# Two expert blocks moved behind the result's copy, with their rows summed on chip

## The chip, the core and the metric

The kernel runs on one core of a Trainium2 chip. A core has engines with an instruction queue each: PE (TensorE: matrix products, with PEld for its weight loads), DVE (VectorE), ACT (ScalarE), POOL (GpSimd) and SP (SyncE, which only starts transfers). Sixteen DMA engines move data between the chip's memory (DRAM) and the on-chip memory (SBUF). The engines run on their own and meet through semaphores. The metric is the device time of the whole program in microseconds (us), measured per execution; the median of the executions is what is compared.

## The reference

A layer of a graph network on 3125 nodes with 256 features. A graph part and a mixing part are added to `x`; then each node passes through two of eight expert networks, and their weighted results are added:

```python
x = x + gnn(xn, edges) + mix(xn)
xt = layernorm(x)
probs = softmax(xt @ Wr + br)                 # 8 experts
top_p, top_idx = top_k(probs, 2)
weights = top_p / top_p.sum(-1)
xe = norm(xt) * ln_g[e] + ln_b[e]             # for each expert e
h = gelu(xe @ W1[e] + b1[e])                  # 256 -> 1024
y = h @ W2[e] + b2[e]                         # 1024 -> 256
out = x + sum over the two chosen e of weights[e] * y[e]
```

Everything is in float32. What matters here is the last sum: a node's result is its row of `x` plus two expert rows, which come from two different experts, and so at two different times.

## The kernel before

Up to about 715 us the kernel computes the graph and mixing parts (lines 215 to 770). For 25 tiles of 126 nodes it then stores the sum so far into `acc_dram`, a DRAM tensor of 3125 + 128 rows (L773), finds the two experts of each node, and scatters the node's normalised row, with its eight expert weights and its number, into `xs_dram` (L872). There every expert has a region of its own, filled beforehand with blank rows whose number is 3125 (`blank`, L491 to 493), so that the results of unused slots go to the spare rows of `acc_dram`.

A plan (from L897) counts the rows that each expert holds, and lists blocks of 256 rows (`SB`): each of the eight experts has a first block with a fixed place, and what goes beyond is listed in `begin_i`, `who_i` (whole blocks) and `hbegin_i`, `hwho_i` (half blocks of 128). `used_i` holds how many of each the plan came to.

The expert stage is the function `block` (from L969), called 28 times in a row: first the eight fixed blocks, then sixteen listed ones, and after each four of these one half block. A call

- loads the two weight matrices of its expert, 1 MB each (L992, L993), and a bias (L995); the buffers of these are three deep (`ew`);
- loads its rows `xs` from `xs_dram` (L1006; three buffers). A listed block takes place and expert from registers, which SP reads from the plan (L985);
- transposes the rows on PE (L1010), scales them on DVE into `xe` (L1014; two buffers), multiplies by the first matrix with a GELU on ACT (L1020, L1022), and by the second (L1033), in halves of 128 rows;
- for each half adds the bias (L1036), multiplies by the row's weight (L1037), and adds the 128 rows into `acc_dram` with an indirect DMA that POOL issues (L1038). It adds in memory, and each of these waits until the one before has landed, since both may touch one row.

After the 28 calls come blocks that this input does not need, under three `If`s (L1049 to L1055) on `used` and `hused`, which every engine reads from `used_i` into a register (L1047, L1048). An engine that skips a body still has to raise the semaphores that the body would have raised. The last line copies `acc_dram` to `out` (L1056, 3.2 MB).

The kernel is written with a framework (Tile) that places the semaphores and chooses the order of each engine's queue from a plan of its own, in which an instruction goes out when its inputs and buffers are free; the order of the queues is therefore not that of the text. By hand an order can be asked for: `tc.issue_after(ins)` keeps what is written under it behind `ins` on the same engine, and `tc.add_manual_dep` makes one instruction wait for another. `declare_no_dep` drops waits between the members of a group.

Of the kernel before, what the change touches and what calls it, by code (L numbers as in the profile page):

```python
# [9 lines left out]
F32 = mybir.dt.float32  # L10
I32 = mybir.dt.int32
# [3 lines left out]
OP = mybir.AluOpType  # L15
AX = mybir.AxisListType

N = 3125
C = 256
# [10 lines left out]
NE = 8  # L30
HID = 1024
KF = HID // 128
# [10 lines left out]
SURE = 2 * N // SB  # L43
HSURE = NE // 2
# [19 lines left out]
def gps_layer(  # L64
# [9 lines left out]
    nc = tc.nc  # L74
# [11 lines left out]
    def ps_tr():  # L86
        return psum.tile([128, 512], F32, tag="tr", name="ps_tr", bufs=2)
# [17 lines left out]
    acc_dram = dram.tile([N + 128, C], F32, name="acc_dram")  # L105
# [385 lines left out]
    blank = mp.tile([128, ROW], F32, name="blank", bufs=1)  # L491
    nc.gpsimd.memset(blank, 0.0)
    nc.gpsimd.iota(blank[:, C + NE:].bitcast(I32), pattern=[[0, 1]], base=N, channel_multiplier=1)
    xs_b = xs_dram.rearrange("(n p) c -> p n c", p=128)
    nb = XROWS // 128
    FILL = 53
# [4 lines left out]
    nh = TB * HEADS  # L501
# [392 lines left out]
    with tc.tile_pool(name="plan", bufs=1) as lp:  # L894
# [63 lines left out]
        nc.vector.tensor_scalar(hgone, hwho[:, :, 0], float(NE - 1), None, op0=OP.min)  # L958
        hwho_i = keep.tile([128, NE], I32, name="hwho_i")
        nc.vector.tensor_copy(hwho_i, hgone)  # L960
        used_i = keep.tile([128, 2], I32, name="used_i")
        nc.vector.tensor_copy(used_i[:, 0:1], ends[:, 0, NE - 1:])
        nc.vector.tensor_copy(used_i[:, 1:2], hends[:, 0, NE - 1:])


    SP = (mybir.EngineType.SP,)
    NH = SB // 128
    with tc.tile_pool(name="ffn", bufs=2) as fp:
        def block(b, half=False):  # L969

            nh = 1 if half else NH
            ns = 128 * nh
            if b < NE and not half:
                begin, e = b * R, b
                xs_b, w1_b, w2_b = xs_dram[begin:begin + SB, :], W1[e], W2[e]
                b2_b = b2[e:e + 1, :]
                is_e = None
            else:
                if half:
                    of, is_e = (hbegin_i, hwho_i), is_hwho[:, b:b + 1, :]  # L980
                    j = b
# [12 lines left out]
            b2s = ew.tile([128, C], F32, name="b2s")  # L994
            nc.sync.dma_start(b2s, b2_b.to_broadcast([128, C]))  # L995
            if is_e is None:
                sm = small[:, :, b]
            else:
                all_ = fp.tile([128, KS, NE], F32, name="all_")
                nc.vector.tensor_tensor(all_, small,  # L1000
                                        is_e.to_broadcast([128, KS, NE]), OP.mult)
                sm = fp.tile([128, KS], F32, name="sm")
                nc.vector.tensor_reduce(sm, all_, AX.X, OP.add)
            lng, lnb, b1s = sm[:, :KC], sm[:, KC:2 * KC], sm[:, 2 * KC:]
            xs = fp.tile([128, NH, ROW], F32, name="xs", bufs=3)[:, :nh, :]
            nc.sync.dma_start(xs, xs_b.rearrange("(h p) c -> p h c", p=128))  # L1006
            pt = ps_tr()
            for k in range(KC):
                for h in range(nh):
                    nc.tensor.transpose(pt[:, k * ns + h * 128:k * ns + h * 128 + 128],  # L1010
                                        xs[:, h, 128 * k:128 * k + 128], ident)
            xe = fp.tile([128, KC, SB], F32, name="xe")[:, :, :ns]
            for k in range(KC):
                nc.vector.tensor_scalar(xe[:, k, :], pt[:, k * ns:(k + 1) * ns],  # L1014
                                        lng[:, k:k + 1], lnb[:, k:k + 1], op0=OP.mult, op1=OP.add)
            hf = fp.tile([128, KF, SB], F32, name="hf")[:, :, :ns]
            for m in range(KF):
                pm = ps_mm()[:, :ns]
                for k in range(KC):
                    nc.tensor.matmul(pm, w1[:, k, 128 * m:128 * m + 128], xe[:, k, :],  # L1020
                                     start=(k == 0), stop=(k == KC - 1))
                nc.scalar.activation(hf[:, m, :], pm, AF.Gelu, bias=b1s[:, m:m + 1])  # L1022
            for h in range(nh):
                if is_e is None:
                    gate = xs[:, h, C + e:C + e + 1]
                else:
                    gate = fp.tile([128, 1], F32, name="gate", bufs=4)
                    scr = fp.tile([128, NE], F32, name="scr", bufs=4)
                    nc.vector.scalar_tensor_tensor(scr, xs[:, h, C:C + NE], 1.0, is_e[:, 0, :],  # L1029
                                                   op0=OP.mult, op1=OP.mult, accum_out=gate)  # L1030
                po = ps_o()[:, :C]
                for m in range(KF):
                    nc.tensor.matmul(po, hf[:, m, 128 * h:128 * h + 128], w2[:, m, :],  # L1033
                                     start=(m == 0), stop=(m == KF - 1))
                y = fp.tile([128, C], F32, name="y", bufs=4)
                nc.vector.tensor_tensor(y, po, b2s, OP.add)  # L1036
                nc.vector.tensor_scalar(y, y, gate, None, op0=OP.mult)  # L1037
                nc.gpsimd.indirect_dma_start(  # L1038
                    out=acc_dram[:, :],
                    out_offset=bass.IndirectOffsetOnAxis(ap=xs[:, h, C + NE:].bitcast(I32), axis=0),  # L1040
                    in_=y, in_offset=None, compute_op=OP.add)

        for b in range(SURE):
            block(b)
            if b >= NE and (b - NE) % HSURE == HSURE - 1:
                block((b - NE) // HSURE, half=True)
        used = nc.values_load(used_i[0:1, 0:1], min_val=0, max_val=ND)  # L1047
        hused = nc.values_load(used_i[0:1, 1:2], min_val=0, max_val=NE)  # L1048
        for b0, b1 in ((SURE, SURE + 2), (SURE + 2, NBLK)):  # L1049
            with tc.If(used > b0 - NE):  # L1050
                for b in range(b0, b1):
                    block(b)
        with tc.If(hused > HSURE):
            for b in range(HSURE, NE):
                block(b, half=True)  # L1055
    nc.sync.dma_start(out, acc_dram[:N, :])  # L1056


# [57 lines left out]
```

## Time and profile before

| | |
|---|---|
| median of 3 runs | 1149.16 us (1146.96 to 1151.12) |
| the profiled execution, its time | 1149.45 us |
| its span (first to last instruction) | 1147.7 us |
| granted PE clock, mean of the span | 0.968 |
| PE busy | 1057.1 us (92%) |
| DVE, ACT, POOL busy | 553.6, 427.5, 169.7 us |
| a whole block on PE: L1020, L1033 | 7.07 us each |
| a half block on PE: L1020, L1033 | 3.73, 3.62 us |
| adding DMA (L1038): POOL's time, start to landing | 1.54 us; 3.7 / 4.2 / 7.7 us (shortest, median, longest) |
| scatter into `xs_dram` (L872): the same | 0.98 us; 2.6 / 2.8 / 10.0 us |
| gather into `near` (L283): the same | 0.97 us; 3.1 / 4.2 / 5.3 us |
| last adding DMA starts | 1126.5 us |
| copy to `out` is issued | 1133.7 us |

How to read it: the page shows busy times of the engines, not who waits for whom. A busy time counts towards the span only where nothing else runs beside it. Of the stage of interest the useful views are the timeline of one engine, whose brackets give the idle time before an instruction and what ended it; the waits of an engine's queue; and, for one line of the program, the list of its queue events (branches, semaphore steps, drains), which are not counted as busy. The 40-slice rows of the page show the end of the program at a glance:

```profile
PE   5799999999999999999999998299999999899992
...
DMA  7884965963007521213121111157666676666734
```

In these rows a slice is 28.7 us. PE is at nine tenths or more through the expert stage, and in the last slice, where the copy runs, at two.

### The profile page before, as it was taken

To read this page: it belongs to the slowest core of one execution; us is meant where nothing else is said; L and a number is where in the kernel's file an instruction comes from. 1 tells how busy PE (TensorE), PEld (TensorE's weight loads), DVE (VectorE), ACT (ScalarE), POOL (GpSimd) and SP (SyncE) were. 2 spreads that over 40 slices of the span, in tenths; PEclk is the share of its full clock that TensorE was granted. 3 is DMA by queue.
4 is the path that set the end of the run, shared out by engine and by line. 5 is a ranking of instruction groups with operands and counts; after the bars stand their busy time and mean duration, and the time that the engine had idled before them with its cause. 6 is when DMAs were issued, how large, how long until landed. Compare 5 with 4: busy or idle time off the path is not lost. (4 is left out here: it accounts for less than half of the span.)

```text
span 1147.7 us, 15551 instructions
## 1 busy us (share of the span) xinstructions
PE 1057.1 (92%) x5613; PEld 807.3 (70%) x5613; DVE 553.6 (48%) x1767; ACT 427.5 (37%) x936; POOL 169.7 (15%) x153
## 2 busy tenths in 40 slices
PE   5799999999999999999999998299999999899992
PEld 2357988988996454545454557288888888788881
DVE  5757788788761184848383937411112222222210
ACT  3454755755732233334333336122222232222220
POOL 2220000000001002020202021212212222122221
PEclk9889999999999999999999999599999999999996
DMA  7884965963007521213121111157666676666734
GB/s 230 293 278 131 252 168 130 253 170 96 1 1 239 176 91 38 91 38 91 38 91 37 36 38 46 52 147 201 188 193 189 187 235 184 201 188 193 227 65 126
DMA packets 121148, 161.43 MB, mean 141 GB/s; under 512 B 9570, under 2 KB 109320, under 8 KB 120870
## 3 DMA queue, kind: packets, MB, share of 16 engines
q1 hardware_dynamic: 108156, 144.40, 41.0%
q0 software_dynamic: 12064, 15.08, 7.1%
q8 instruction: 49, 0.80, 0.3%
q10 hardware_dynamic: 840, 0.83, 0.2%
q14 instruction: 39, 0.32, 0.1%
HBM read 101.37 MB, written 62.10 MB: 142 GB/s over the span
## 5 line engine op out<-in xcount | busy, mean ns | idle before, releaser
L747 PE MATMUL ps_mm<-hT,wih 128*128 128x504 f32 (+1 forms) x672 | 257.8, 543 | 1.6 <-ACT act L749 1.6
L747 PEld LDWEIGHTS ps_mm<-hT,wih 128*128 128x128 f32 x672 | 120.3, 190 | 133.8 <-issue 127.9
L1020 PE MATMUL ps_mm<-xe,w 128*128 128x256 f32 (+1 forms) x896 | 189.4, 369 | 3.3 <-DVE xe L1014 3.3
L1033 PE MATMUL ps_o<-w,hf 128*128 128x256 f32 x832 | 184.2, 379 | 0.0
L1020 PEld LDWEIGHTS ps_mm<-xe,w 128*128 128x128 f32 x896 | 161.6, 192 | 27.0 <-DVE xe L1014 6.6
L630 PE MATMUL ps_o<-A,hi 126*128 126x252 f32 (+1 forms) x650 | 176.3, 305 | 0.8 <-ACT A L392 0.7
L1033 PEld LDWEIGHTS ps_o<-w,hf 128*128 128x128 f32 x832 | 157.8, 190 | 21.3
L630 PE MATMUL ps_o<-A,lo 126*128 126x252 f32 (+1 forms) x650 | 161.2, 281 | 0.0
L1022 ACT ACTIVATE hf<-ps_mm,sm 128x256 f32<-128x256 f32 (+1 forms) x160 | 71.7, 453 | 199.2 <-PE ps_mm L1020 197.5
L392 ACT CAST A<-ps_mm 126x450 fp32r<-126x450 f32 x175 | 93.8, 538 | 99.8 <-PE ps_mm L390 98.2
L1038 POOL DMA_INDIRECT acc_dram<-y,xs x52 | 80.4, 1546 | 318.8 <-DVE scr L1029 131.6
L630 PEld LDWEIGHTS ps_o<-A,hi 126*128 126x128 f32 x650 | 124.9, 192 | 2.8 <-ACT aggT L638 1.7
L384 DVE TENSOR_TENSOR hr<-two,rowT 128x756 bf16<-128x756 bf16 x175 | 95.9, 548 | 62.9 <-PE ps_mm L390 62.4
L630 PEld LDWEIGHTS ps_o<-A,lo 126*128 126x128 f32 x650 | 125.2, 193 | 0.0
L390 PE MATMUL ps_mm<-hk,hr 128*126 128x150 bf16 x1050 | 102.2, 233 | 12.7 <-DVE hk L384 12.4
L384 DVE TENSOR_TENSOR hk<-two,keyT 128x900 bf16<-128x900 bf16 x175 | 108.8, 622 | 0.0
L390 PEld LDWEIGHTS <-hr 128*126 128x126 bf16 x1050 | 91.2, 137 | 18.7 <-DVE hk L384 16.5
L1036 DVE TENSOR_TENSOR y<-ps_o,b2s 128x256 f32<-128x256 f32 x52 | 22.1, 425 | 163.9 <-PE ps_o L1033 163.9
L749 ACT ACTIVATE act<-ps_mm,bg 128x504 f32<-128x504 f32 (+1 forms) x84 | 52.6, 634 | 107.3 <-PE ps_mm L747 107.2
L795 DVE SCALAR_TENSOR_TENSOR scr<-xl,wrows 126x256 f32<-126x256 f32 x160 | 75.5, 472 | 3.3
L872 POOL DMA_INDIRECT xs_dram<-rows,at_i x50 | 52.6, 1052 | 127.9 <-DVE at_i L869 110.9
L1022 ACT ACTIVATE hf<-ps_mm,small 128x256 f32<-128x256 f32 x64 | 29.8, 474 | 76.4 <-PE ps_mm L1020 76.4
(250 smaller groups left out, 920.1 us busy)
## 6 DMA issues: line engine op xcount, KB each, us to landing
w<-in_W_dram SPq DMA_DIRECT2D x56, 1024.0 KB
xs_dram<-blank SPq DMA_DIRECT2D x3, 7022.5 KB
xs_dram<-blank SPq DMA_DIRECT2D x1, 6757.5 KB
xs<-xs_dram SPq DMA_DIRECT2D x24, 265.0 KB
root_dram<-hr SPq DMA_DIRECT2D x24, 252.0 KB
root<-root_dram SPq DMA_DIRECT2D x6, 1008.0 KB
b2s<-in_b_dram SPq DMA_DIRECT2D x28, 128.0 KB
xn_dram<-xn SPq DMA_DIRECT2D x5, 630.0 KB
```

Source lines behind the costliest of these rows:

```text
L384: row = nc.vector.tensor_tensor(to[:, :m], two[:, :, :w, :].to_broadcast([128, m, w, GH]), of[:, g:g + m, None, :].to_broadcast([128, m, w ...
L390: mm = nc.tensor.matmul(pa[:P, i * DT:(i + 1) * DT], hr[:, i, :, h], hk[:, i, :, h], start=(h == 0), stop=(h == GH - 1))
L392: copy = nc.scalar.copy(A[:, :, c0:c0 + m * D], pa[:P, :m * DT].rearrange("p (d t) -> p t d", t=T))
L630: last = nc.tensor.matmul(pg[k][:, :n], of[:, t, 128 * k:128 * k + 128], A[:, t, :n], start=(t == 0 and of is hi), stop=(t == T - 1 and of ...
L747: mm = nc.tensor.matmul(pm[:, :n], wih[:, k, i, 128 * m:128 * m + 128], hT[:, k, :n], start=(k == 0), stop=(k == KH - 1))
L749: nc.scalar.activation(act[:, i, :n], pm[:, :n], AF.Tanh if gate == 2 else AF.Sigmoid, bias=bg[:, gate, m:m + 1])
L795: nc.vector.scalar_tensor_tensor(scr, xl[:, i, :], 1.0, wrows[:, e, :], op0=OP.mult, op1=OP.mult, accum_out=lg[:, i, e:e + 1])
L872: put = nc.gpsimd.indirect_dma_start(out=xs_dram[:, :], out_offset=bass.IndirectOffsetOnAxis(ap=at_i[:w, i:i + 1], axis=0), in_=rows[:w, i ...
L1020: nc.tensor.matmul(pm, w1[:, k, 128 * m:128 * m + 128], xe[:, k, :], start=(k == 0), stop=(k == KC - 1))
L1022: nc.scalar.activation(hf[:, m, :], pm, AF.Gelu, bias=b1s[:, m:m + 1])
L1033: nc.tensor.matmul(po, hf[:, m, 128 * h:128 * h + 128], w2[:, m, :], start=(m == 0), stop=(m == KF - 1))
L1038: nc.gpsimd.indirect_dma_start(out=acc_dram[:, :], out_offset=bass.IndirectOffsetOnAxis(ap=xs[:, h, C + NE:].bitcast(I32), axis=0), in_=y, ...
```

## The change

- The loop of 28 calls leaves out the blocks of experts 6 and 7; they are called after it, with `last=True`.
- The first of the two, in its own body, copies `acc_dram` to `out`: the copy now stands ahead of their results. It waits for all the adding DMAs before it.
- A `last` block gathers, for its 256 rows, what has been summed so far into `old`: expert 6 from `acc_dram`, expert 7 from `out`, after expert 6's rows have landed there. The gather from `out` leaves out rows whose number is beyond 3124, hence the `memset`.
- In place of the multiplication and the adding DMA, one DVE operation forms `y * gate + old`, and an indirect DMA without addition stores the rows in `out`. Each waits for the copy; among each other they don't wait. Expert 7's gathers wait for expert 6's stores.
- The plan also counts `more`: whether there are whole blocks beyond the sixteen or halves beyond the four. If so, the results of experts 6 and 7 are also added to `acc_dram` in the old way, the further blocks run as before, and `acc_dram` is copied to `out` once more at the end. These are two new `If`s, one ahead of the three and one behind.
- The registers are read behind the last matmul, the last row operation and the last stores of their engines.
- The spare rows of `acc_dram` are set to zero once, in the mixing stage.

```diff
@@ in the mixing stage
     nc.gpsimd.iota(blank[:, C + NE:].bitcast(I32), pattern=[[0, 1]], base=N, channel_multiplier=1)
+    nc.sync.dma_start(acc_dram[N:, :], blank[:, :C])
@@ in the plan
-        used_i = keep.tile([128, 2], I32, name="used_i")
-        nc.vector.tensor_copy(used_i[:, 0:1], ends[:, 0, NE - 1:])
-        nc.vector.tensor_copy(used_i[:, 1:2], hends[:, 0, NE - 1:])
+        used_f = lp.tile([128, 3], F32, name="used_f")
+        nc.vector.tensor_copy(used_f[:, 0:1], ends[:, 0, NE - 1:])
+        nc.vector.tensor_copy(used_f[:, 1:2], hends[:, 0, NE - 1:])
+        spill = lp.tile([128, 2], F32, name="spill")
+        for i, sure in enumerate((SURE - NE, HSURE)):
+            nc.vector.tensor_scalar(spill[:, i:i + 1], used_f[:, i:i + 1], -float(sure), 0.0,
+                                    op0=OP.add, op1=OP.max)
+        nc.vector.tensor_tensor(used_f[:, 2:], spill[:, 0:1], spill[:, 1:2], OP.add)
+        used_i = keep.tile([128, 3], I32, name="used_i")
+        nc.vector.tensor_copy(used_i, used_f)
@@ in block(b, half=False, last=False), after the load of xs
+            if last:
+                if not done:
+                    done.append(nc.sync.dma_start(out, acc_dram[:N, :]))
+                old = fp.tile([128, NH, C], F32, name="old", bufs=2)
+                sums, most = (acc_dram, None) if len(done) == 1 else (out, N - 1)
+                if most:
+                    nc.vector.memset(old, 0.0)
+                for h in range(nh):
+                    get = nc.gpsimd.indirect_dma_start(
+                        out=old[:, h, :], out_offset=None, in_=sums[:, :],
+                        in_offset=bass.IndirectOffsetOnAxis(
+                            ap=xs[:, h, C + NE:].bitcast(I32), axis=0),
+                        bounds_check=most, oob_is_err=False)
+                    for put in done[1:]:
+                        after(get, put)
@@ in block, after y = po + b2s
+                ys.append(y)
+                if not last:
+                    nc.vector.tensor_scalar(y, y, gate, None, op0=OP.mult)
+                    add(y, h, xs)
+                    continue
+                new = fp.tile([128, C], F32, name="new", bufs=2)
+                row = nc.vector.scalar_tensor_tensor(new, y, gate, old[:, h, :], op0=OP.mult, op1=OP.add)
+                put = nc.gpsimd.indirect_dma_start(
+                    out=out[:, :],
+                    out_offset=bass.IndirectOffsetOnAxis(ap=xs[:, h, C + NE:].bitcast(I32), axis=0),
+                    in_=new, in_offset=None, bounds_check=N - 1, oob_is_err=False)
+                tc.declare_no_dep(put.ins, group="lasts", reason="rows of their own")
+                tc.add_to_no_dep_group("lasts", put.ins)
+                after(put, done[0])
+                puts.append(put)
+            done.extend(puts)
+            return xs, ys, (*puts, row, mm) if last else ()
@@ the calls
-        for b in range(SURE):
+        done = []
+        for b in (*range(NE - 2), *range(NE, SURE)):
             block(b)
             if b >= NE and (b - NE) % HSURE == HSURE - 1:
                 block((b - NE) // HSURE, half=True)
-        used = nc.values_load(used_i[0:1, 0:1], min_val=0, max_val=ND)
-        hused = nc.values_load(used_i[0:1, 1:2], min_val=0, max_val=NE)
+        lasts = [block(b, last=True) for b in (NE - 2, NE - 1)]
+        with ExitStack() as queued:
+            for ins in lasts[-1][2]:
+                queued.enter_context(tc.issue_after(ins.ins))
+            used, hused, more = [nc.values_load(used_i[0:1, i:i + 1], min_val=0, max_val=ND)
+                                 for i in range(3)]
+        with tc.If(more > 0):
+            for e, (xs, ys, _) in zip((NE - 2, NE - 1), lasts):
+                for h in range(NH):
+                    nc.vector.tensor_scalar(ys[h], ys[h], xs[:, h, C + e:C + e + 1], None,
+                                            op0=OP.mult)
+                    add(ys[h], h, xs)
...
-    nc.sync.dma_start(out, acc_dram[:N, :])
+        with tc.If(more > 0):
+            again = nc.sync.dma_start(out, acc_dram[:N, :])
+            for put in done:
+                after(again, put)
```

`add(y, h, of)` is the adding DMA of before (L1038) as a function; `after(ins, of)` makes `ins` wait for `of` with `tc.add_manual_dep`.

More of the change, by code (lines that the diff above doesn't have):

```diff
@@ L968, in gps_layer, with add, block @@
     with tc.tile_pool(name="ffn", bufs=2) as fp:
-        def block(b, half=False):
+        def add(y, h, of):
+            nc.gpsimd.indirect_dma_start(
+                out=acc_dram[:, :],
+                out_offset=bass.IndirectOffsetOnAxis(ap=of[:, h, C + NE:].bitcast(I32), axis=0),
+                in_=y, in_offset=None, compute_op=OP.add)
+        def block(b, half=False, last=False):
             nh = 1 if half else NH
@@ L1006, in block @@
             nc.sync.dma_start(xs, xs_b.rearrange("(h p) c -> p h c", p=128))
+            if last:
[13 more added lines that the diff above has]
+                        after(get, put)
+            ys, puts = [], []
             pt = ps_tr()
@@ L1032, in block, with after @@
                 for m in range(KF):
-                    nc.tensor.matmul(po, hf[:, m, 128 * h:128 * h + 128], w2[:, m, :],
-                                     start=(m == 0), stop=(m == KF - 1))
+                    mm = nc.tensor.matmul(po, hf[:, m, 128 * h:128 * h + 128], w2[:, m, :],
+                                          start=(m == 0), stop=(m == KF - 1))
                 y = fp.tile([128, C], F32, name="y", bufs=4)
                 nc.vector.tensor_tensor(y, po, b2s, OP.add)
-                nc.vector.tensor_scalar(y, y, gate, None, op0=OP.mult)
-                nc.gpsimd.indirect_dma_start(
-                    out=acc_dram[:, :],
-                    out_offset=bass.IndirectOffsetOnAxis(ap=xs[:, h, C + NE:].bitcast(I32), axis=0),
-                    in_=y, in_offset=None, compute_op=OP.add)
-        for b in range(SURE):
+                ys.append(y)
[7 more added lines that the diff above has]
+                    out=out[:, :],
+                    out_offset=bass.IndirectOffsetOnAxis(ap=xs[:, h, C + NE:].bitcast(I32), axis=0),
+                    in_=new, in_offset=None, bounds_check=N - 1, oob_is_err=False)
[5 more added lines that the diff above has]
+            return xs, ys, (*puts, row, mm) if last else ()
+        def after(ins, of):
+            tc.add_manual_dep(ins.ins, of.ins.name, mybir.DependencyInfo(
+                mybir.DependencyClass.Sync, mybir.DependencyReason.DATA), reason="rows of one another")
+        done = []
+        for b in (*range(NE - 2), *range(NE, SURE)):
             block(b)
```

## The prediction

> **What bounds the kernel now.** I read the page's group table first, then the TensorE (PE) timeline of the expert stage, then the tail after the last matmul; the change touches only the last two. From 740 us to 1125.4 PE runs the 28 calls of `block` almost without a break:
>
> ```profile
> L1020 PE MATMUL ps_mm<-xe,w 128*128 128x256 f32 (+1 forms) x896 | 189.4, 369 | 3.3 <-DVE xe L1014 3.3
> L1033 PE MATMUL ps_o<-w,hf 128*128 128x256 f32 x832 | 184.2, 379 | 0.0
> ```
>
> The last figures are PE's idle time before those lines: 3.3 and 0.0 us. So a term counts only if it opens a gap on PE or lies behind its last matmul. The PE timeline has one real gap. Columns are start, length, what, and in brackets the idle time and its releaser:
>
> ```profile
> 981.95 3.73 PE L1020 MATMUL ps_mm<-xe,w 128*128 128x128 f32 x32
> 985.52 3.62 PE L1033 MATMUL ps_o<-w,hf 128*128 128x256 f32 x16
> 988.98 0.60 PE L1010 MATMUL ps_tr<-ident,xs 128*128 128x128 f32 x4
> 992.72 0.67 PE L1010 MATMUL ps_tr<-ident,xs 128*128 128x128 f32 x4 [3.15 <-DMA xs<-xs_dram]
> 993.75 8.59 PE L1020 MATMUL ps_mm<-xe,w 128*128 128x256 f32 x32 [0.35 <-DVE xe L1014]
> ...
> 1067.17 7.07 PE L1033 MATMUL ps_o<-w,hf 128*128 128x256 f32 x32
> 1074.08 1.04 PE L1010 MATMUL ps_tr<-ident,xs 128*128 128x128 f32 x8
> 1075.32 7.17 PE L1020 MATMUL ps_mm<-xe,w 128*128 128x256 f32 x32 [0.20 <-DVE xe L1014]
> ```
>
> Transposes run in pairs of calls: eight (or six, with a half) stand ahead of the first call's L1020. At 992.72 the pair's second `xs` was not there. `xs` has three buffers, so it is loaded only after the scatter of three calls earlier has landed: that scatter started at 984.34, 2.2 us after its block's last matmul, and landed at 989.87; the load was issued at 989.96 and arrived at 992.7. Normally two further whole blocks cover this; here one of the two was a half block, 7 us instead of 14.
>
> The tail is this: the SyncE waits (line, what it waited for, total, times, longest), then events of the tail by line (durations, first and last start):
>
> ```profile
> SPq L1056 <- DMA acc_dram<-y,xs: 31.1, 1, 31.1
> SPq L1112 <- DMA out_dram<-acc_dram: 11.7, 1, 11.7
> ```
>
> ```profile
> L1050 PEldq COMPARE_BRANCH  x2: 2287/3610/4933, 1123.8 to 1126.3; - x2
> ...
> L1050 POOLq INC_SWDGE_SEM  x2: 915/916/917, 1127.7 to 1131.1; - x2
> ```
>
> ```profile
> L1053 PEldq COMPARE_BRANCH  x1: 2642/2642/2642, 1131.9 to 1131.9; - x1
> ```
>
> ```profile
> L1112 POOLq DRAIN  x3: 46/107/3139, 1133.7 to 1147.4; - x3
> ...
> L1112 PEldq DRAIN  x2: 8/8/8, 1140.7 to 1147.2; - x2
> ```
>
> Last matmul 1125.4; last scatter 1126.5, landed 1131.1 (POOL's own wait on it ends there). The copy starts only at 1133.7: POOL (GpSimd) walks three skipped `If`s, each with a 0.92 us semaphore step, and the copy waits for the last one. It ends at 1146.5, 12.7 us later, and 1.2 us of closing steps end the span. From last matmul to end: 22.3 us.
>
> **The change, part by part.**
>
> *The copy moved forward.* It is issued after the 26th call's scatter. Number the calls 0 to 27: halves were 12, 17, 22, 27 and become 10, 15, 20, 25; blocks 6 and 7 become 26 and 27. Call T0 the end of call 25. Its scatter starts at T0+1.1 and lands 4.6 later (tail rows), so the copy runs from T0+5.8 to T0+18.5, beside some 33 us of PE work. Gain: the 12.7 us leave the tail, and so does the wait before them. If uncovered, they come back whole.
> It is queued on SyncE, where it could hold up block 7's loads. This queue does not follow the program's text: the weights of the first blocks were issued at 360 to 377 us, before inputs that stand earlier in the code, and the read of `used` at 726.3, before the first `xs` at 736.9. What is ready goes first. Block 7's weights are free to load when call 24 releases its buffers and its `xs` when that call's scatter lands, 13 and 6 us ahead of the copy; so I put the copy behind them, at no cost.
>
> *A new gap.* Call 24 is a block, 25 a half, (26, 27) a pair: the same pattern as (16, 17), (18, 19) now. The old gap recurs at (16, 17), whose predecessor 15 is a half. Today the fourth half ends the chain and nothing follows it; now a pair does. Price from the rows: from the half's end to L1020 4.61 us (989.14 to 993.75) against 1.08 (1074.24 to 1075.32), +3.53; and that L1020 took 8.59 against 7.17, +1.42: together **+4.95**. [...] Bounds: 0, if the queue puts block 7's transposes later; 7, if the landing takes the 7.7 us that is the longest of these scatters.
>
> *Gathers, sums and plain stores* in blocks 6 and 7. Four gathers, no row with 1 KB rows from this place: nearest are `near` (0.97 us of POOL, 4.2 to landing) and the plain store `xs_dram` (0.99, 2.8). Four plain stores replace four adding scatters (1.54, 4.2). I take 1.0 and 2.8, ends 1.0/2.8 and 1.5/4.2. Block 6's gathers go at T0+5.8; even slowed to 8 us by the copy they precede the first new sum at T0+16.8. Its stores wait for the copy (T0+18.5) and for its last row (T0+21.3, with the gap); landed at T0+24 to 25.5; block 7's gathers wait behind them on POOL and land at T0+28 to 31.4. They are needed at T0+34.4. Three us spare, cost 0. Without the gap the need is at T0+30.4, and up to 1 us shows. The `new` operation is 0.47 us (a 126x256 SCALAR_TENSOR_TENSOR row, L795) instead of 0.35: +0.12 in the tail. The `old` memset and the missing gate multiply are off the path.
>
> *Plan and blank store.* About four DVE operations of 0.15 us more, ending near 730.6 instead of 730.0, and a third register load of some 0.7 us on SyncE; the first `xs` waits for scatters until 736.5 anyway. Without that cover, 1.3 us. The 128 KB store to `acc_dram` goes out some 300 us before anyone adds there: 0.
>
> *The tail.* Two more skipped `If`s, and the third register load on each engine. From the last matmul, in us:
> POOL: rows, sum and issue of the last store 1.0; eight waits of 0.085, 1.7; three loads of 0.38, 2.9; four skips of 1.6 (1127.35 to 1128.94 is one), 9.3; 0 to 0.6 more if the last store lands after the second skip asks for it; the fifth, which has no GpSimd work, 0.3: about 9.9; DRAIN 3.1: **13.0**.
> PE: now its third branch ends 9.2 after the last matmul. One load more and two near branches make 9.9. Its DRAIN came 6.1 us later, behind a 16 KB instruction packet that started only at 1138.2, amid the copy; such a packet otherwise costs 2.3 to 2.6 us (the 2.29 and 2.64 rows), so 12.4.
> Then 0.85 of closing: **13.8 instead of 22.3**, gain 8.5. [...] Ends of the tail: 10.5 if POOL's DRAIN shrinks and PE has its last packet early; 15.5 if both new `If`s cost PE 0.8 each.
>
> **Sum.** +4.95 − 8.5 = −3.6 us (3.55). Span 1147.7 → 1144.1. The profiled execution took 1149.45, 1.75 around its span; so 1145.9, and the runs' median lies 0.29 below that execution: **1145.6 us**, 0.31% under the median of 1149.16. The gain of the copy is half eaten by the pattern it creates.
>
> **Rivals.**
> *No new gap.* If the transposes of 27 stand behind L1020 of 26, or its `xs` comes early, only the tail counts: −8.5, 1140.7. For it: blocks 6 and 7 need no register-read addresses. Against it: the half/pair pattern is the same, and `xs` still waits for a scatter.
> *The chain copy, store, gather, store becomes late.* For it: four dependent transfers, and adding scatters took up to 7.7 us, `xs_dram` stores up to 10. If block 6's last store takes 7.7 and block 7's gather 10, its rows come at T0+40.5 rather than 34.4: +6.1, 1151.7; at half that excess, 1148.7. It decides once the gathers land after T0+34.4.
> *The copy stands ahead of block 7's loads on SyncE*: the slower side. SyncE then sits in its wait until T0+5.8; weights and `xs` (2.4 MB) queue behind the copy to T0+18.5 and at some 0.35 MB/us land near T0+25.5. Since the pair's transposes wait for that `xs`, block 6 itself starts at T0+26.5 rather than T0+4.6: +22, 1167. It decides as soon as block 7's `xs` arrives later than T0+3.6; each us after that is a us. Against it: the order by readiness shown above.
>
> **From these to the numbers.** Forecast 0.50, own range 1142.5 to 1148.5; no gap 0.22 (1138.5 to 1142.5); late chain 0.16 (1148.5 to 1154); queue order 0.08; others, slower, 0.04. The bound of 0.3% is 3.4 us, about what a measurement of this kernel can tell from no change, so faster means under 1145.7: half of the first case and the second, 0.47. Within: the other half and half of the third, 0.33. Slower: 0.20. Range 1139 to 1152: all of the first, most of the second, half of the third.
>
> **What would show it.** Copy issued about 30 us before the last matmul and ended before block 7's first L1020 is half done; SyncE's loads of block 7 before it; a PE wait of 3 us for `xs` ahead of block 6, and L1020 of 8.6 after it; DVE never waiting for `old` in block 7; the end 13 to 14 us after the last matmul, with POOL's DRAIN and PE's nearly together. It is wrong if DVE or POOL waits on gathers at the end, if PE's branches take other times, or if the pairing changes.

## The result, and the profile after

| | before | after |
|---|---|---|
| median of the runs | 1149.16 us (5 runs, 1146.96 to 1151.12) | 1142.23 us (5 runs, 1138.13 to 1143.33) |
| profiled execution, its span | 1149.45, 1147.7 us | 1143.33, 1141.5 us |
| granted PE clock, mean | 0.968 | 0.972 |
| last matmul ends | 1125.39 us | 1128.30 us |
| from there to the end | 22.3 us | 13.2 us |

By the medians that is 6.9 us less, where 3.6 was forecast (1145.6 us); the ratio of the runs is 0.9931, with an interval of 0.9909 to 0.9954, which is 5.3 to 10.5 us. The profiled execution is the slowest of the five of after, so the traces account for 6.2 us and not 6.9.

The PE row of the page, 40 slices of 28.5 us:

```profile
PE   5799999999999999999999998199999998999995
```

The last digit was 2 and is 5. The one 8 among the last 9s is the old gap: it stood a slice later in the row of before, where the expert stage was at 9 but for this slice and the last. The new gap is too short to lower its digit. The PE timeline of the changed kernel shows it: first the place where the old gap now is, then the end of the stage. Columns are start, length, what, idle time and its releaser.

```profile
955.56 3.62 PE L1067 MATMUL ps_o<-w,hf 128*128 128x256 f32 x16
959.01 0.60 PE L1044 MATMUL ps_tr<-ident,xs 128*128 128x128 f32 x4
962.94 1.12 PE L1044 MATMUL ps_tr<-ident,xs 128*128 128x128 f32 x4 [3.33 <-DMA xs<-xs_dram]
963.96 9.76 PE L1054 MATMUL ps_mm<-xe,w 128*128 128x256 f32 x32
```

```profile
1093.16 3.62 PE L1067 MATMUL ps_o<-w,hf 128*128 128x256 f32 x16
1096.62 0.60 PE L1044 MATMUL ps_tr<-ident,xs 128*128 128x128 f32 x4
1100.01 0.66 PE L1044 MATMUL ps_tr<-ident,xs 128*128 128x128 f32 x4 [2.80 <-DMA xs<-xs_dram]
1100.50 7.07 PE L1054 MATMUL ps_mm<-xe,w 128*128 128x256 f32 x32
...
1121.23 7.07 PE L1067 MATMUL ps_o<-w,hf 128*128 128x256 f32 x32
```

L1044, L1054 and L1067 are the L1010, L1020 and L1033 of before. A second wait for `xs` has appeared, ahead of the pair of blocks 6 and 7, and nothing else interrupts PE until it is done: no wait for a weight, a gather or the copy.

SyncE's queue shows why the copy (L1027) disturbs nothing. Block 7's two weights (L1008, L1009), bias (L1011) and rows (L1022) are all issued ahead of it:

```profile
1082.88 0.37 SPq L1008 DMA_DIRECT2D w<-in_W_dram  x1
1089.78 0.37 SPq L1009 DMA_DIRECT2D w<-in_W_dram  x1
1090.24 0.54 SPq L1011 DMA_DIRECT2D b2s<-in_b_dram  x1
1097.39 0.37 SPq L1022 DMA_DIRECT2D xs<-xs_dram  x1
1102.18 0.60 SPq L1027 DMA_DIRECT2D out_dram<-acc_dram  x1
```

POOL's timeline of the same stretch holds the chain of gathers (L1033) and plain stores (L1079):

```profile
1102.43 1.04 POOL L1033 DMA_INDIRECT old<-acc_dram,xs  x1 [2.54 <-DMA acc_dram<-y,xs]
1103.77 0.98 POOL L1033 DMA_INDIRECT old<-acc_dram,xs  x1 [0.31 <-issue]
1115.50 1.02 POOL L1079 DMA_INDIRECT out_dram<-new,xs  x1 [10.75 <-DVE y L1070]
1116.82 1.00 POOL L1079 DMA_INDIRECT out_dram<-new,xs  x1 [0.30 <-issue]
1120.44 1.04 POOL L1033 DMA_INDIRECT old<-out_dram,xs  x1 [2.62 <-issue]
1121.79 1.03 POOL L1033 DMA_INDIRECT old<-out_dram,xs  x1 [0.30 <-issue]
1126.26 1.00 POOL L1079 DMA_INDIRECT out_dram<-new,xs  x1 [3.44 <-DVE new L1078]
1129.56 1.00 POOL L1079 DMA_INDIRECT out_dram<-new,xs  x1 [2.29 <-DMA out_dram<-new,xs]
```

The last store starts 1.26 us after the last matmul's end: the two DVE operations behind that matmul end at 1129.28, 0.28 us before the store. The bracket names another releaser, the landing of the store before (1129.45), which came at nearly the same time; in e9 below the distance is the same 1.27 us, and there the bracket names `new`. DVE's waits agree that no gather was late: it waited for `old` once, 3.1 us in block 6 by this view, which cost PE nothing, and never in block 7.

```profile
DVE new L1078 <- DMA old<-acc_dram,xs: 3.1, 1, 3.1
```

The tail, in the queue events of the skipped `If`s and of the end, by line (durations shortest, median, longest; first and last start):

```profile
L1107 POOLq INC_SWDGE_SEM  x1: 1022/1022/1022, 1131.0 to 1131.0; - x1
```

```profile
L1114 PEldq COMPARE_BRANCH  x2: 430/1904/3378, 1126.2 to 1128.5; - x2
...
L1114 POOLq INC_SWDGE_SEM  x2: 983/994/1006, 1132.8 to 1134.3; - x2
```

```profile
L1117 PEldq COMPARE_BRANCH  x1: 4068/4068/4068, 1132.5 to 1132.5; - x1
...
L1117 POOLq INC_SWDGE_SEM  x1: 1001/1001/1001, 1136.0 to 1136.0; - x1
```

```profile
L1179 POOLq DRAIN  x3: 51/107/3466, 1137.2 to 1141.3; - x3
...
L1179 PEldq DRAIN  x2: 8/8/8, 1137.1 to 1141.0; - x2
```

POOL pays four semaphore steps of about 1.0 us, one for each skipped body that has GpSimd work, then, from 1137.2, the DRAIN of 3.47 us. PE is through its five branches at 1137.1, 3.5 us before POOL's DRAIN ends: POOL sets the end.

The account of the two profiled executions, span 1147.7 to 1141.5, from the timelines:

| | forecast | measured |
|---|---|---|
| stage begins (738.25, was 739.96), its first 12 matmuls (4.80 us, was 4.00) | 0 | −0.9 |
| the old gap at its new place (wait 3.33, L1054 9.76; were 3.15 and 8.59) | 0 | +1.3 |
| the new gap: 1096.78 to 1100.50 is 3.72, less the normal 1.08, and L1054 0.1 shorter than normal | +4.95 | +2.5 |
| the tail | −8.5 | −9.1 |
| sum | −3.6 | −6.2 |

### The profile page after: what moved, and what is told of

Its sections match the earlier page's. It is cut to its first block, busy times and chain, and to the rows that moved or that the text cites. A ratio compares the mean times of both kernels' runs of the same rounds, so it can differ in the third digit from the quotient of the medians.

```text
span 1141.5 us, 15590 instructions
## 1 busy us (share of the span) xinstructions
PE 1057.0 (93%) x5613; PEld 808.4 (71%) x5613; DVE 554.5 (49%) x1772; ACT 427.2 (37%) x936; POOL 171.0 (15%) x157
## 5 line engine op out<-in xcount | busy, mean ns | idle before, releaser
L1054 PE MATMUL ps_mm<-xe,w 128*128 128x256 f32 (+1 forms) x896 | 191.2, 372 | 2.7 <-DVE xe L1048 2.7
L1067 PE MATMUL ps_o<-w,hf 128*128 128x256 f32 x832 | 184.2, 379 | 0.0
L1054 PEld LDWEIGHTS ps_mm<-xe,w 128*128 128x128 f32 x896 | 163.1, 194 | 26.7 <-DVE xe L1048 5.8
L1067 PEld LDWEIGHTS ps_o<-w,hf 128*128 128x128 f32 x832 | 158.0, 190 | 21.1
L980 POOL DMA_INDIRECT acc_dram<-y,xs x48 | 74.2, 1546 | 298.6 <-DVE scr L1063 131.8
L390 PE MATMUL ps_mm<-hk,hr 128*126 128x150 bf16 x1050 | 102.3, 233 | 12.6 <-DVE hk L384 12.4
```

What stands on the lines that cost most here:

```text
L390: mm = nc.tensor.matmul(pa[:P, i * DT:(i + 1) * DT], hr[:, i, :, h], hk[:, i, :, h], start=(h == 0), stop=(h == GH - 1))
L980: nc.gpsimd.indirect_dma_start(out=acc_dram[:, :], out_offset=bass.IndirectOffsetOnAxis(ap=of[:, h, C + NE:].bitcast(I32), axis=0), in_=y, ...
L1067: mm = nc.tensor.matmul(po, hf[:, m, 128 * h:128 * h + 128], w2[:, m, :], start=(m == 0), stop=(m == KF - 1))
```

## The experiments

My account was: the copy in mid-stage is free, the new pattern of pairs opens a gap on PE, the tail is POOL's walk over skipped `If`s. The rivals: the order of calls costs nothing and the tail did all of it; the copy or the gathers hold the last blocks up; PE's branches bound the tail. e6 and e7 leave out the `If`s of the end, whose bodies this input doesn't need. The kernel before was measured again beside each set of experiments (1149.58, 1148.23 and 1148.06 us), the kernel after was not: a distance from after is taken from the medians, or from the two ratios to before.

### e1: only the order of the calls, on the kernel before

```diff
-        for b in range(SURE):
+        for b in (*range(NE - 2), *range(NE, SURE)):
             block(b)
...
+        for b in (NE - 2, NE - 1):
+            block(b)
```

> The kernel before, with the blocks of experts 6 and 7 run last, but still added with the adding DMA, and the copy still at the end. My account (the copy's 12.7 us and the wait before it left the tail; the reorder alone costs a gap on PE ahead of the last pair): the tail stays near 22 us, a new gap of 2.5 to 5 us opens ahead of block 6, so about +2.5 to +5 us over the kernel before, 1152 to 1154. Rival (the reorder itself brings the gain, the copy was hidden anyway): about 1142, as the changed kernel.

1153.35 us against 1149.58, ratio 1.0033 (1.0022 to 1.0044). The order alone costs 3.8 us, and its trace shows the second gap, with nearly the wait and the matmuls (3.15, 8.59) that the prediction had taken from the first:

```profile
1098.62 0.85 PE L1010 MATMUL ps_tr<-ident,xs 128*128 128x128 f32 x4 [3.16 <-SPq L1052]
1099.27 8.60 PE L1020 MATMUL ps_mm<-xe,w 128*128 128x256 f32 x32
```

The releaser named here is a queue event of SyncE; its own waits name the adding DMAs for the load of `xs` (L1006), as in before:

```profile
SPq L1006 <- DMA acc_dram<-y,xs: 6.7, 1, 6.7
```

So the gap belongs to the order, and neither the copy nor the gathers make it.

### e2, e5: one half ahead of its block

A half that stands ahead of the block it used to follow is no longer the call that ends just before a pair, and two whole blocks cover the scatter again. In e2 this is done for the fourth half in the kernel after, in e5 for the second half in the kernel before (there `first` is `(b - NE) // HSURE == 1`).

```diff
+            here = b >= NE and (b - NE) % HSURE == HSURE - 1
+            first = here and b == SURE - 1
+            if first:
+                block((b - NE) // HSURE, half=True)
             block(b)
-            if b >= NE and (b - NE) % HSURE == HSURE - 1:
+            if here and not first:
                 block((b - NE) // HSURE, half=True)
```

> The changed kernel with the fourth half block run ahead of its whole block, so that it is the first of its pair (24, 25) and not the second. My account (a half as the second call of a pair leaves too little time for the next pair's second xs): the 2.80 us wait ahead of block 6 goes, the last matmul comes about 2.5 us earlier, time about 1139.7. Rival (block 6 starts late for its weights, or because blocks 6 and 7 are where they are): the gap stays, 1142.

> The kernel before, with the second half block alone run ahead of its whole block. My account: the one gap of the kernel before goes, 3.53 us of gap and 1.42 us of slowed matmuls: -4.95, about 1144.2, with the same tail of 22.3 us. Rival (the gap belongs to that place in time, not to the half's place in its pair): 1149.

e2: 1137.05 us, ratio 0.9886 (0.9862 to 0.9909); the new gap is gone from the trace and the old one stays (2.53 us of waiting). That is 5.2 us under after, twice what I had expected from the one trace of after. Part of it lies outside the gap: in e2's trace the old gap was itself shorter than in after's. e5: 1144.92 us against 1148.23, ratio 0.9968 (0.9956 to 0.998), no gap left: the same move is worth 3.3 us in the kernel before, less than the 4.95 expected.

### e3, e4: both gaps removed, in two ways

e3 puts the second and the fourth half ahead. e4 keeps every call where it is and gives `xs` a fourth buffer:

```diff
-            xs = fp.tile([128, NH, ROW], F32, name="xs", bufs=3)[:, :nh, :]
+            xs = fp.tile([128, NH, ROW], F32, name="xs", bufs=4)[:, :nh, :]
```

> The changed kernel with the second and the fourth half ahead of their whole blocks. My account: both gaps go (in the profile of the changed kernel 6.3 us at the second half with the slowed matmuls behind it, 2.5 at the fourth): about 8.8 us, time about 1133.5. Rival: 1142, or 1139.7 if only one of the two gaps has this cause.

> The changed kernel with four xs buffers instead of three; PE's order is the same. My account: the load of xs then waits for the scatter of four calls earlier, so both gaps go although the halves stand as second of their pairs: about 8.8 us less, about 1133.5. Rival (weights or the order itself make the gap): no change, 1142.

1133.96 us (ratio 0.9859, 0.9835 to 0.9883) and 1134.89 us (0.9865, 0.9842 to 0.9887). A buffer does what a reordering does, so the gap is the wait for an `xs` buffer and no property of a half as such. At the old place e4 still waits 0.68 us, with no slowed matmuls behind it. At the new place its PE runs through without the wait:

```profile
1088.30 3.62 PE L1067 MATMUL ps_o<-w,hf 128*128 128x256 f32 x16
1091.75 1.04 PE L1044 MATMUL ps_tr<-ident,xs 128*128 128x128 f32 x8
1092.99 7.17 PE L1054 MATMUL ps_mm<-xe,w 128*128 128x256 f32 x32 [0.20 <-DVE xe L1048]
```

e3 showed a new thing. Its last matmul ends at 1116.98, but the tail is 15.6 us, not 13.2. POOL's timeline of e3:

```profile
1113.03 1.04 POOL L1033 DMA_INDIRECT old<-out_dram,xs  x1 [2.94 <-issue]
1114.38 1.03 POOL L1033 DMA_INDIRECT old<-out_dram,xs  x1 [0.30 <-issue]
1119.20 1.00 POOL L1079 DMA_INDIRECT out_dram<-new,xs  x1 [3.79 <-DVE new L1078]
1120.51 1.00 POOL L1079 DMA_INDIRECT out_dram<-new,xs  x1 [0.30 <-issue]
```

Block 7's gathers are still in flight when its sums are due. The last store starts 3.5 us after the last matmul instead of 1.26, and DVE waits for them:

```profile
DVE new L1078 <- DMA old<-out_dram,xs: 3.1, 2, 2.1
```

Of the 2.3 us, DVE's wait before the last sum is 1.0. The rest is POOL: it issued block 7's first store at 1119.20, though its sum was ready at 1116.54, and the last one 1.3 us after it. So the chain copy, store, gather, store has little to spare once the gap is gone, 3.4 us in after (second gather landed 1125.43, last sum begun 1128.80), while in e3 it came 1.0 us too late. It need not show: the last store starts 1.27 us after the last matmul in e4, and 1.34 in e2, whose order at the end is that of e3. These are single executions; what makes the gathers land later in some wasn't isolated.

### e6, e7: no `If`s at the end

The register loads and the `If`s behind the calls are removed, three in the kernel before (e6) and five in the kernel after (e7).

> The kernel before without the register loads and the three Ifs behind the 28 calls (this input needs none of their bodies). My account: the copy starts when the last adding DMA has landed, near 5.7 us after the last matmul instead of 8.3, and ends 12.7 us later: -2.6 us and little more, about 1146.5. Rival (the skipped Ifs set PE's and POOL's end, hidden behind the copy): 1149.

> The changed kernel without the register loads and the five Ifs behind the last block (this input needs none of their bodies). My account (POOL's walk through four skips and its drain set the end 13.2 us after the last matmul): the end comes when the last plain store has landed and the closing steps are done, 4.2 + 1.2 us after the last matmul, or 3 us later if POOL's drain stays long: 5.4 to 8.5 us of tail, about 5 to 8 us less than 1142, 1134 to 1137. Rival (the chain copy, store, gather, store sets the end): 1142.

e6: 1144.22 us against 1148.23, ratio 0.9956 (0.994 to 0.9972), 4.0 us less, tail 18.1 instead of 22.3. That is more than the 2.6 us expected: the copy was issued 4.9 us after the last matmul, where it was 8.3 in before and 5.7 in my sum. e7: 1135.43 us, ratio 0.9889 (0.9865 to 0.9913), tail 6.6 instead of 13.2. The `If`s are worth 4.2 us of the tail in the kernel before, where they delay the copy, and 6.6 in the kernel after. Without any `If` the tails differ by 11.5 us, close to the copy's 12.7: so what the change could win in the tail is about the copy. It won 9.1; the other 2.4 us is the 6.6 less the 4.2, and after has two skips and a third load more to pay for (no run took out these alone). POOL sets the end in e7 too:

```profile
L1157 POOLq DRAIN  x3: 51/113/4709, 1125.8 to 1131.1; - x3
```

This DRAIN looks longer than the 3466 ns of after, but it starts while the last store is still on POOL. It ends at 1130.5, and that is 3.5 us after the store's end at 1127.03.

### e8: the copy ahead of block 7's loads on SyncE

```diff
+            behind_ = ExitStack()
+            if last and done:
+                behind_.enter_context(tc.issue_after(done[0].ins))
...
             xs = fp.tile([128, NH, ROW], F32, name="xs", bufs=3)[:, :nh, :]
             nc.sync.dma_start(xs, xs_b.rearrange("(h p) c -> p h c", p=128))
+            behind_.close()
```

> The changed kernel with block 7's four loads held behind the copy in SyncE's queue; PE then has block 7's transposes behind block 6's matmuls. My account: the copy waits for the last half's scatter, the 2.4 MB of block 7 run behind the copy, xs lands some 25 us after the end of the last half, so block 6 runs without its gap and block 7 starts about 11 us late: the last matmul about 9 us later than in the changed kernel, 1151. Rival (the loads share the DMA engines with the copy and come in time): 1142.

1151.78 us against 1148.23, ratio 1.0034 (1.0023 to 1.0045). This is the rival on the slower side, made real: the same copy in the same stage, 9.5 us dearer than in after by the medians and 11.8 by the ratios, through its place in a queue. The profiled execution is the slowest of its 22 (1158.23 us), so its waits may be longer than usual. SyncE's timeline and PE's in e8:

```profile
1083.32 0.37 SPq L1025 DMA_DIRECT2D xs<-xs_dram  x1
1103.57 0.61 SPq L1031 DMA_DIRECT2D out_dram<-acc_dram  x1
...
1105.41 10.76 SPq L1014 DMA_DIRECT2D b2s<-in_b_dram  x1
1116.27 0.68 SPq L1025 DMA_DIRECT2D xs<-xs_dram  x1
```

```profile
1106.28 7.07 PE L1071 MATMUL ps_o<-w,hf 128*128 128x256 f32 x32
1125.24 1.11 PE L1048 MATMUL ps_tr<-ident,xs 128*128 128x128 f32 x4 [11.89 <-SPq L1118]
1127.00 9.29 PE L1058 MATMUL ps_mm<-xe,w 128*128 128x256 f32 x32 [0.64 <-DVE xe L1052]
```

SyncE stands in the copy's wait for 20 us. Then the loads queue up behind the copy (the issue of the bias alone lasts 10.76 us), and block 7's transposes wait 11.9 us for rows whose load was issued at 1116.27; a landing at 1125.20 in the trace, 0.04 us before the transposes start, fits it, and the releaser named is only the queue event that came last. Block 6 is not held up: the framework put block 7's transposes behind it here, so a pair is no fixed thing.

### e9, e10, e11: two `If`s instead of five

All bodies behind the first `If` (further blocks, halves, the second copy) go under one condition, `more > 0`, and only `more` is read. If it held, all of the further blocks would run, needed or not; no run here had such an input:

```diff
-            used, hused, more = [nc.values_load(used_i[0:1, i:i + 1], min_val=0, max_val=ND)
-                                 for i in range(3)]
+            more = nc.values_load(used_i[0:1, 2:3], min_val=0, max_val=ND)
...
-        for b0, b1 in ((SURE, SURE + 2), (SURE + 2, NBLK)):
-            with tc.If(used > b0 - NE):
-                for b in range(b0, b1):
-                    block(b)
-        with tc.If(hused > HSURE):
+        with tc.If(more > 0):
+            for b in range(SURE, NBLK):
+                block(b)
             for b in range(HSURE, NE):
                 block(b, half=True)
-        with tc.If(more > 0):
             again = nc.sync.dma_start(out, acc_dram[:N, :])
```

e10 adds the fourth `xs` buffer of e4, e11 the two halves of e3.

> After, with the three conditions behind the adds' If and the last one drawn into one If on the same value, so that two skips follow the last plain store and two register loads are gone. My account: everything up to the last matmul as in after (about 1128.3). POOL's part of the tail loses three skips of about 1.6 us and part of the loads, so the tail falls from 13.2 to 7.8 to 9.3 us and the median from 1142.2 to 1137 to 1138.5. Rival A (PE's branches over the enlarged body set the end instead): PE's branches over the two bodies of after that took 3.4 and 4.1 us grow or stay, PE ends after POOL, the tail stays above 10.5. Rival B (what POOL pays belongs to its queue, not to the skips): the time of the skips turns up in the DRAIN behind them, the tail stays at 13.

> The run before this one (two Ifs) with a fourth buffer for xs. My account: no PE gap in the experts' stage (as e4), last matmul near 1121 to 1122, the last plain store within 2 us of it, tail as in the run before this: 1127 to 1130.5 us. If the two savings are not independent (the chain of the last gathers comes late once the gaps are gone), up to 2.5 us more: 1133.

> Two Ifs with the second and fourth half ahead of their blocks. My account: last matmul as in e3 (about 1117), the late chain keeps its 2.3 us, tail 10 to 11.7 us instead of 15.6, 1128.5 to 1130.5 us; level with the run before this within 1.5 us. If the chain of gathers is what decides alone, the two Ifs gain the same here as in after (4 to 5.4 us off e3's 1134.0).

| | median | ratio to before | last matmul | tail |
|---|---|---|---|---|
| e9 | 1136.57 us | 0.9906 (0.988 to 0.9933) | 1124.02 | 10.2 us |
| e10 | 1131.26 us | 0.9858 (0.9835 to 0.9881) | 1120.85 | 10.2 us |
| e11 | 1133.28 us | 0.9879 (0.9859 to 0.9899) | 1119.02 | 12.4 us |

In all three the tail is 3 us shorter than with five `If`s (e9 against after, e10 against e4, e11 against e3). The whole times agree only in part: by the ratios e9 is 2.9 us under after, e10 0.8 us under e4, and e11 2.3 us over e3, with intervals of 2 to 3 us on either side, so the 3 us rest on the tails of the traces. That is less than the 4 to 5.4 I had expected: the second skip, at 1127.8 to 1129.8 in e9, took 2.0 us, where two of after with no register load among them took 1.3 and 1.4. The end of e9 by line:

```profile
L1112 PEldq COMPARE_BRANCH  x1: 3608/3608/3608, 1121.6 to 1121.6; - x1
```

```profile
L1175 POOLq DRAIN  x3: 51/107/3466, 1129.8 to 1133.9; - x3
...
L1175 PEldq DRAIN  x2: 7/8/8, 1125.4 to 1133.6; - x2
```

Neither rival holds. PE's branch over the merged body takes 3.6 us, about half of what the separate ones took together in after (0.43, 3.4 and 4.1 us), and PE's DRAIN comes 4.4 us ahead of POOL's. And POOL's DRAIN is the same 3466 ns after two skips as after five, so the skips' time has not moved into it.

e10 has the lowest median of all the kernels, 16.8 us under the kernel before; its ratio, 0.9858, is not to be told from e3's 0.9859 and e4's 0.9865. Against the change it is 11 us by the medians and 8 by the ratios. e11, which removes the gaps by order, keeps the late chain (its last store starts 4.2 us after the last matmul). Against e3 it gained only 0.7 us by the medians, and nothing by the ratios, although its tail is 3.2 us shorter: its profiled execution began the expert stage 2.0 us later (738.44 against 736.42). The begin of the stage lies between 736.4 and 740.0 in the traces, for reasons that lie before it and stay open.

## Why the prediction was right, and where it was not

*The copy moved forward, at no cost*: right. It ran 12.5 us beside PE's work, behind block 7's loads on SyncE as the order by readiness had suggested. e8 shows that this was no small point: the other order would have cost some 10 us and turned the gain into a loss. The rival's price of 22 us was too high, because it took for granted that block 6 waits for block 7's transposes. Its 0.35 MB/us was an estimate: two full stretches of before moved 378 GB/s (1134 to 1140, the copy) and 391 GB/s (993.24 to 996.65), and in e8 block 7's rows landed 21.6 us after the copy's issue, where that sum has 19.7.

*The new gap, +4.95 us*: the mechanism was right, as e1 (order alone, +3.8 us), e2 and e4 show; the size is the term that missed. The profiled execution has +2.5, 2.4 us less, in two parts. The wait itself was 2.80 us, not 3.15, and `xe` was ready at once (a fixed block's gate takes no DVE operation, and DVE was free): from the half's end to L1054 3.72 us, 0.9 less than the row I took. And the L1054 after it took 7.07 us, not 8.59: 1.5 less. When the matmuls were slowed can be read from the profile by stretches of time, here around the old and the new gap of after. The columns are the stretch and its length; busy us (and instructions) of PE, PEld, DVE, ACT and POOL; the granted PE clock; DMA share and GB/s:

```profile
959.00:962.41 3.41, 0.61 (x5) 0.36 (x3) 0.00 (x0) 0.00 (x0) 0.00 (x0) 1.00 0.41 101
962.41:965.82 3.41, 2.88 (x8) 2.23 (x9) 2.69 (x10) 0.00 (x0) 1.38 (x1) 0.50 0.98 372
...
1095.53:1098.94 3.41, 1.69 (x10) 1.26 (x8) 1.68 (x4) 0.00 (x0) 0.60 (x1) 1.00 0.28 53
1098.94:1102.36 3.42, 2.35 (x13) 2.15 (x14) 1.48 (x3) 0.30 (x1) 0.94 (x1) 1.00 0.50 92
```

The stretches are cut at instants a whole number of 3.41 us apart, since that is where the clock changed: in the traces of before and after all changes of the granted clock, 13 in each, lie on such instants. A wait can fall into one such stretch or across two. Here are all waits of 2 to 4 us for `xs` in the traces, with the stretch in which PE was busy least:

| trace | wait, us | PE busy in the emptiest stretch, us | granted clock in the next | the 32 matmuls after the wait, us |
|---|---|---|---|---|
| e1, new gap | 3.16 | 0.32 | 0.50 | 8.60 |
| before | 3.15 | 0.52 | 0.50 | 8.59 |
| after, old gap | 3.33 | 0.61 | 0.50, twice | 9.76 |
| e1, old gap | 3.00 | 0.80 | 0.50 | 8.15 |
| e2, old gap | 2.53 | 0.88 | 0.50 | 8.54 |
| e6 | 2.28 | 0.99 | 0.50 | 8.73 |
| e9, new gap | 2.38 | 1.19 | 0.50 | 8.76 |
| e7, new gap | 2.22 | 1.29 | 0.50 | 8.76 |
| e8, old gap | 3.12 | 1.35 | 0.50 | 8.86 |
| after, new gap | 2.80 | 1.69 | 1.00 | 7.07 |
| e7, old gap | 2.65 | 1.72 | 1.00 | 7.17 |
| e9, old gap | 2.57 | 1.78 | 1.00 | 7.17 |
| e8, at 1044.57 | 2.52 | 1.90 | 1.00 | 7.17 |

The length of the wait does not sort the last column: of the waits of 2.2 to 2.8 us four had slowed matmuls behind them (2.22 to 2.53) and four had not (2.52 to 2.80). The third column does. With 0.32 to 1.35 us of work in a stretch the next one ran at 0.50, with 1.69 to 1.90 us at 1.00. That is what these waits show, and not a limit for the whole span: in after a stretch with 1.92 us of work, from 88.60, was followed by 0.50, and one with 1.80 us, from 150.04, by 1.00. Where the instants lie in a wait differs from one execution to the next: 3.15 us of waiting in before left 0.52 us of work in the emptiest stretch, 3.12 us in e8 left 1.35. So a wait of 2.2 to 2.8 us was followed by slowed matmuls in some traces and not in others, and the 1.42 us, which I had from one row, should have stood in the forecast as a share, with 0 as its lower end. In the old gap at its new place they cost more than before (+1.3 us in all), as the clock stayed at 0.50 for a second stretch (965.82 to 969.23). The experiments, which average over it, put a gap at 3.8 us (e1), 5.2 (e2) and, for the old gap in before, 3.3 (e5): the 4.95 lies at their upper end.

*Gathers and stores hidden*: right for this kernel, with a different margin. Beside the copy the first of block 6's gathers took 12.2 us, from its start at 1102.43 until `new` ran at 1114.59, not the 8 I had allowed; both of block 7's, with the copy done, took 5.0 (1120.44 to 1125.43). It cost nothing since block 6's stores wait for the copy anyway. The step "without the gap up to 1 us shows" was too small: e3 shows 2.3 us and e11 3.0, while e2, e4 and e10 show 0.1 at most.

*Plan and blank store, at no cost*: nothing in the trace speaks against it; the stage began 1.7 us earlier than before, which is within the scatter of the other runs.

*The tail, 13.8 us*: 13.2, right to 0.6 us, but not by the steps given. POOL reached its DRAIN 8.9 us after the last matmul where 9.9 was summed, and the DRAIN took 3.47 where 3.1 was taken. "PE 12.4" fell: PE's DRAIN was reached 8.8 us after the last matmul, with no such wait behind the branches as in before, so the near tie did not exist. In such a tie shortening POOL alone would have won little. No run shortened POOL alone: e9 and e10 shortened PE's walk too, and won 3 us of tail. But PE's DRAIN came 3.5 us before POOL's ended in after, so by this trace POOL alone could have been shortened by about that much before PE set the end. The long branches of PE were taken from before, where they lasted 2287, 4933 and 2642 ns, with 16 KB instruction packets started at 1123.7, 1127.0, 1127.3 and 1132.0, while ScalarE's lasted 45 ns each. In after two of PE's again took 3378 and 4068 ns; the one over two whole blocks took 430, those over a body without matrix work 212 and 224, and DVE's 56 and 67. So PE's long branches came again, but not at every `If`.

The forecast's sum was thus 3.4 us too high by the medians. At 1142.23 the result even lies 0.3 us below the range that I gave to the forecast itself (1142.5 to 1148.5), in the one given to "no new gap", although the gap is there: the number alone would have spoken for the wrong case. In the traces the difference is 2.6 us: 2.4 from the gap, 0.6 from the tail, and the start and the old gap, −0.9 and +1.3, nearly cancel. That these two cancel is luck. What remains is within the scatter of the runs (1138.13 to 1143.33 for after). That the new order eats a good part of the gain stands: e2, the same change without the new gap, gains 12.5 us over before by the medians, after 6.9.

## What to carry to other kernels

When calls are moved, look at what each call's buffers wait for in the new order. Here a rotation of three buffers hid a landing behind two whole blocks and opened waits of 3.33 and 2.80 us where one of the two was a half; a fourth buffer left 0.68 us and none (e4) without a change of order. A long transfer taken from the tail to the middle was free here behind the loads that the next work needs, and cost some 10 us ahead of them (e8), so read the order of the issuing queue first. At the end of a program, count the conditions: skipping five `If`s made the tail 6.6 us longer than none (after against e7), two in place of five made it 3 us shorter (e9), and conditions that this input never meets could share one.

## What the runs showed of the hardware

- In before and after the granted PE clock changed only at instants a whole number of 3.41 us apart. At the waits of the table, a stretch with 0.32 to 1.35 us of PE work was followed by one at 0.50, a stretch with 1.69 to 1.90 us by one at 1.00. In after it stayed at 0.50 for a second stretch, with 2.88 us of work in the first; in before, with 3.06 us in the first, it returned to 1.00.
- A gather of 128 rows of 1 KB took 12.2 us beside a copy of 3.2 MB from DRAM to DRAM; after it two of them took 5.0 from the first one's start. The copy took 12.5 us beside them and 12.7 by itself in the tail of before.
- A skipped body with GpSimd work cost POOL a semaphore step of 0.98 to 1.02 us (0.92 in before). POOL's DRAIN took 3466 ns behind the skips, whether there were five or two; in e7, without any, it ended 3.5 us after the last store's end.
- PE's branch over one merged body (3608 ns in e9 and e10, 3918 in e11) was not longer than the longest over its parts (430, 3378 and 4068 ns).
- With the copy ahead of the loads on SyncE (e8), the issue of one load lasted 10.76 us, where it took 0.54 in after.
